# Layer 1's sums begun before the last block ends, and an opening with a place for each image

## The chip, the cores and the metric

The kernel runs on one core of a Trainium2 chip. The metric is the device time of one execution in microseconds (us). A core has TensorE (matrix products and transposes through PSUM), VectorE (DVE), ScalarE (ACT), GpSimd (POOL) and SyncE (SP, which here only issues DMAs). ACT and POOL issue DMAs too; POOL issues the indirect ones, which gather rows by a list of indices.

## The reference

Two graph layers on N = 3327 nodes with D = 128 features (padded to NP = 3328 = 26 blocks of 128 rows), all in float32. The adjacency has about 2% of entries that are not zero (0.0096 made symmetric, and the diagonal).

```
h = relu(layernorm(x))                                   # layer 0: attention, 4 heads
E = leaky_relu(h@w1 [i] + h@w2 [j]);  s = exp(8*tanh(E@a / 8)) * adj
head = leaky_relu((s / sum_j s) @ h @ Wlin.T);  x = x + concat(heads) @ w
h = relu(layernorm(x))                                   # layer 1: a graph convolution
A = adj + I;  dinv = rowsum(A)**-0.5
x = x + relu(dinv[:,None] * A * dinv[None,:] @ (h @ W.T + b))
```

## The kernel before

**Tables.** An opening (L884 to L1062) norms x, multiplies it with the weights and writes, for each node, a row of ROW = 720 floats to DRAM: 64 places for adjacency weights, 128 features, 4 scores, ones, and from PROJ = 208 on 4 x 128 projections. There are two such tables, one for the upper half of a block's rows (hb = 0) and one for the lower (hb = 1); they differ in the first 64 places only, which are rewritten for each block from AT_d, a transposed copy of the adjacency in DRAM (`weights`, L555, issued on SP). The rows are built in `img` tiles, one for four blocks, 7 in all, from a pool of 5 (L952); `store` (L969) writes each to table 0, and to table 1 one image later. The memory of the opening (pool `pre`) is given back at its end, and the gather buffers `g` (pool `pg`, 4 buffers, opened after it) lie there.

**Layer 0** goes through 26 blocks. For each, `prep` (L338) reads 128 rows of the adjacency (`load`, L336, on SP), transposes them on TensorE (L349), copies them out of PSUM on ACT (L351, tile `at`) and writes them to AT_d (L354), and makes on DVE the lists of the neighbours' indices (idx at L442, and idxo at L511 for those that don't fit). Blocks after the first few also multiply the transposed adjacency at once with those columns of layer 1's input that are known by then (`known_step`, L364) into part1_d.

Each half block has 4 windows of 8 gathers (tile `g`, L548) and one of 3 (`ge`). Two groups come out of a window and one out of `ge`, so 18 groups a block. A group is: 16 transposes of gathered projections into PSUM (`z`, L573; in a ge group also L576), a maximum on DVE (L585; on ACT for ge, L582), score products (L597); then, for a window, a copy on ACT (L605), transposes into a `tr` bank (L614; the `tr` pool has two banks), score additions on DVE (L617, L620), tanh and exp on ACT, weights on DVE, and the weighted sums (L645, for ge L663). `close` (L669) ends each half: for the second it goes over L685, L696, L707, L711, L723, L731 and L736, which writes the block's column of layer 1's input into x_sb and sets `closed`.

**The order** of instructions is the order of emission. `slot` (L808) is called 6 times a group; each call takes one step of every open `finish` and `close`, steps of the next block's `prep`, and calls `fetch` and `trickle`. `fetch` queues the gathers of the next window as soon as a buffer is free by the count in `state`; `trickle` issues from this queue at RATE = 0.7 a slot, and each gather is made to wait for the latest maximum of L585 (the pace). POOL does the gathers in order, SP and ACT their DMAs among their other work.

**Layer 1** multiplies x_sb's 26 columns with strips of AT_d, each four blocks (512 rows of the output) wide; strip s starts at column `finished(4*s)` = 4*s - 2 (0 for s = 0), since the columns before are in part1_d. There are 7 strips with 26, 24, 20, 16, 12, 8 and 4 columns, the last one half as wide. Pieces of 11 columns are loaded into g buffers (`strip`, L820, SP and ACT in turn). `layer1` (L859) takes strip after strip, a matmul 128x512 for each column (L870) into a z bank; it takes the first 25 columns of strip 0 between the last steps of the last block, and stops before column 25 until that is written (`yield "all"`). `strip_out` (L841) adds part1, transposes (L853), scales and adds (L854 to L856) and writes the output.

Of the kernel before, what the change touches and what calls it, by code (L numbers as in the profile page):

```python
# [15 lines left out]
P = 128  # L16
# [47 lines left out]
ROW = 720  # L64
FEAT = 64
PROJ = 208
# [161 lines left out]
def _sparse_layers(tc, nc, x, adj, w1, w2, a, wlin, w, gw, gb, gb_sb, gwT, x_sb, dinv, flag, ident, out):  # L228
# [24 lines left out]
    with ExitStack() as l0:  # L253
# [5 lines left out]
        part1_d = dram.tile([D, NP], F32, name="part1_d")  # L259
        NS = -(-NB // 4)  # L260
# [12 lines left out]
        lower = res.tile([P, P], F32, name="lower")  # L273
        rowid = res.tile([P, 1], F32, name="rowid")
# [16 lines left out]
        nc.gpsimd.iota(epos, [[-P, 2 * OVT]], base=2 * NP, channel_multiplier=-1, allow_small_or_imprecise_dtypes=True)  # L291

# [45 lines left out]
        def prep(b, k):  # L338
# [6 lines left out]
            def tables_step(j0):  # L345
# [4 lines left out]
                at = pat.tile([P, 4, P], F32, name="at") if b else blks[0].pool.tile([P, 4, P], F32, name="at0", bufs=4)  # L350
# [65 lines left out]
            hTb = pb.tile([P, P], F32, name="hTb")  # L416
            nc.sync.dma_start(hTb, hT_d[:, b * P:(b + 1) * P])
# [24 lines left out]
            nc.vector.tensor_scalar(idx, pm[:, :64].rearrange("p (c t) -> p c t", c=4), -1.0, float(NP), op0=OP.mult, op1=OP.add)  # L442
# [68 lines left out]
            nc.vector.tensor_scalar(idxo.rearrange("p c t -> p (c t)"), hits, -1.0, float(NP), op0=OP.mult, op1=OP.add)  # L511
# [23 lines left out]
            k.x1b, k.x1n, k.pex, k.hTb = x1b, x1n, pex, hTb  # L535
            yield

        def gather(b, hb, w):

            k = blks[b]  # L540
            tab = tables[hb]
            if w == NW:
                g, n, at = pe_.tile([P, OVT, ROW], F32, name="ge"), OVT, k.idxo[:, hb]
            else:
                g, n, at = pg.tile([P, WT, ROW], F32, name="g"), WT, k.idx[:, w, WT * hb:WT * hb + WT]

            def one(t):
                return nc.gpsimd.indirect_dma_start(out=g[:, t, :], out_offset=None, in_=tab[:, :],  # L548
                                                    in_offset=bass.IndirectOffsetOnAxis(ap=at[:, t:t + 1], axis=0))
# [12 lines left out]
        def stage_z(k, hb, m, slot):  # L562
# [4 lines left out]
            for hp in range(2):  # L567
# [15 lines left out]
                else:  # L583
                    r0 = HALF * hb + 32 * (m % 2)
                    made = nc.vector.tensor_tensor(r.rearrange("p h (i s) -> p h i s", s=16), z.rearrange("p h (i s) -> p h i s", s=16),  # L585
                                            k.x1n[:, 2 * hp:2 * hp + 2, r0:r0 + 32, None].to_broadcast([P, 2, 32, 16]), OP.max)
                    state["pace"] = made.ins.name
# [167 lines left out]
        state["pace"], state["credit"] = None, 0.0  # L755
        RATE = 0.7
        SYNC = mybir.DependencyInfo(mybir.DependencyClass.Sync, mybir.DependencyReason.DATA)
# [12 lines left out]
        def fetch():  # L770
            while state["fetched"] < len(fetches):
# [5 lines left out]
                if b == NB:  # L777
                    strip(*pieces[w])
# [9 lines left out]
        def issue():  # L788

            what, _, _, make = queue.popleft()  # L790
            made = make()
            if what is not None and state["pace"] is not None:
                tc.add_manual_dep(made.ins, state["pace"], SYNC, reason="pace")

        def trickle():
            state["credit"] = min(2.0, state["credit"] + RATE) if queue else 0.0
            while queue and (state["credit"] >= 1 or queue[0][0] is None):
                state["credit"] -= queue[0][0] is not None
                issue()
# [6 lines left out]
        def slot():  # L806
# [6 lines left out]
            trickle()  # L813


        PIECE = 11
        pieces = [(s, j0, min(PIECE, NB - j0)) for s in range(NS) for j0 in range(finished(4 * s), NB, PIECE)]
        strips = {}

        def strip(s, j0, n):  # L820
            g = pg.tile([P, WT, ROW], F32, name="g")
            v = g.rearrange("p t c -> p (t c)")[:, :n * 4 * P].rearrange("p (j i) -> p j i", j=n)
            w = min(4, NB - 4 * s) * P
            for k, lo in enumerate(range(0, n, 4)):
                hi = min(n, lo + 4)
                eng = nc.scalar if k % 2 else nc.sync
                eng.dma_start(v[:, lo:hi, :w], AT_d[s * NP + (j0 + lo) * P:s * NP + (j0 + hi) * P, :w].rearrange("(j p) i -> p j i", p=P))
            strips[s, j0] = v

        def strip_in(s):  # L830
# [6 lines left out]
            if finished(4 * s):  # L837
                nc.sync.dma_start(r1[:, 0], part1_d[:, rows].rearrange("p (b i) -> p b i", b=n))
            return n, rows, r0, r1

        def strip_out(s, po, n, rows, r0, r1):  # L841

            ot, t, xo = r0[:, 1], r1[:, 1], r0[:, 0]
            po = po[:, :n * P].rearrange("p (b i) -> p b i", b=n)
            if finished(4 * s):
                nc.vector.tensor_add(ot, po, r1[:, 0])
            else:
# [10 lines left out]

        def layer1():  # L859
            ending = []  # L860
            for s in range(NS):
                w = min(4, NB - 4 * s) * P
                po = ps_z.tile([P, 2, BANK], F32, name="z")[:, 0]
                j1 = finished(4 * s)
                ins = strip_in(s)
                for j in range(j1, NB):
                    if j == NB - 1 and s == 0:
                        yield "all"
                    at = (j - j1) % PIECE
                    nc.tensor.matmul(po[:, :w], x_sb[:, j, :], strips[s, j - at][:, at, :w], start=(j == j1), stop=(j == NB - 1))  # L870
                    if at == PIECE - 1 or j == NB - 1:
                        allow("g")
                    while ending and next(ending[0], "end") == "end":
                        ending.pop(0)
# [355 lines left out]
```

## Time and profile before

| | |
|---|---|
| time, median of 17 executions | 3149.91 us (3137.22 to 3160.67) |
| the profiled execution | 3138.63 us, span 3136.9 us, mean granted TensorE clock 0.915 |
| busy in the span: PE, DVE, POOL, ACT | 81%, 65%, 57%, 22% |
| DMA | 867.74 MB, 277 GB/s on average; gathers take 65.0% of the 16 engines' time |
| first gather issued, first z transpose | 85.6 us, 89.8 us |
| a steady block, 18 groups | 111.6 us |
| a gather of 128 rows on POOL | 0.976 us busy, one in 1.25 us; landing 4.4 us after its issue (median) |
| a gathered window's last row before its first transpose | 13.5 us (median) |
| last group's z transposes end | 3017 us |
| column 25 of strip 0 | 3051.07 us |
| L870 | 220 records (two a column), 96.4 us busy |

The page shows one execution. Busy time is that of instructions in work, an engine's idle time is put down to what ended it, and the chain of waits is followed back from the last instruction. "Another core or an unknown queue" (remote) stands where the trace doesn't hold the releaser. A granted clock below 1 means that TensorE was throttled in part of that stretch.

### The profile page before, as it was taken

Reading aid. Unit: us, or ns where it says so; the run is one execution under the profiler, and the core shown is the slowest. Engines: PE = TensorE matmul, PEld = TensorE weight load, DVE = VectorE, ACT = ScalarE, POOL = GpSimd, SP = SyncE. Lnnn points to the kernel's source line nnn. Section 1 sums busy time; section 2 is a strip of 40 time slices with the busy share of each in tenths; the row PEclk is TensorE's granted clock in tenths of the full one; section 3 lists DMA queues with packets and bytes.
Section 4 is the critical chain, followed back from the end, with each engine's and each line's share of the span. In section 5 each row is a group of like instructions: output and inputs, shape, how many; then the busy total and the mean of one; then the engine's idle time right before and its main releaser. Section 6 shows DMA issues by size and latency. Waiting matters only on the chain.

```text
span 3136.9 us, 52428 instructions
## 1 busy us (share of the span) xinstructions
PE 2527.3 (81%) x19410; PEld 1751.5 (56%) x19410; DVE 2052.6 (65%) x6256; ACT 691.1 (22%) x1648; POOL 1793.8 (57%) x1865
## 2 busy tenths in 40 slices
PE   5478878878878877888888888788888888887888
PEld 3355555555555555655565565566555556555544
DVE  6466767677677767767676666776666666765432
ACT  3122222122222212222222221222222222221110
POOL 2456665665666666666665656656566555656610
PEclk8799999999999999998999998999899999999899
DMA  9888988898899888888988888888898888988876
GB/s 331 267 284 256 287 289 260 285 296 281 268 287 308 265 286 290 285 262 285 296 264 286 288 253 285 285 275 269 279 283 269 276 286 252 293 257 250 254 254 237
DMA packets 459767, 867.74 MB, mean 277 GB/s; under 512 B 208876, under 2 KB 317936, under 8 KB 456176
## 3 DMA queue, kind: packets, MB, share of 16 engines
q0 software_dynamic: 145600, 671.04, 65.0%
q1 hardware_dynamic: 217360, 136.76, 15.6%
q10 hardware_dynamic: 96544, 56.50, 5.9%
q8 instruction: 156, 2.56, 0.3%
q14 instruction: 107, 0.88, 0.1%
HBM read 795.84 MB, written 112.63 MB: 290 GB/s over the span
## 4 chain that ended last, share of the span: by engine, by line
PE 50%; DVE 11%; another core or an unknown queue 10%; issue 6%; ACT 5%; ACTq 0%; DMA 0%; DVEq 0%
PE z L573 19%; PE s L597 9%; DVE r L585 5%; PE tr L614 4%; PE z L870 3%; PE z L576 3%; PE ag L645 2%; PE ag L663 2%; PE tr L364 2%; ACT r L582 2%; PE tr L349 1%; ACT ssb L605 1%; PE tr L496 1%; PE tr L696 1%
## 5 line engine op out<-in xcount | busy, mean ns | idle before, releaser
L548 POOL DMA_INDIRECT g<-table,idx x1664 | 1623.7, 976 | 1075.9 <-issue 431.9
L573 PE MATMUL z<-ident,g 128*128 128x128 f32 x6656 | 1023.6, 300 | 273.3 <-issue 133.8
L585 DVE TENSOR_TENSOR r<-z,x1n 128x1024 f32<-128x1024 f32 x832 | 1011.4, 1217 | 243.5 <-remote 99.4
L573 PEld LDWEIGHTS z<-ident,g 128*128 128x128 f32 x6656 | 839.5, 155 | 479.3 <-issue 236.1
L597 PE MATMUL s<-r,sel 128*32 128x512 f32 (+1 forms) x3744 | 537.9, 616 | 7.9 <-issue 6.4
L617 DVE TENSOR_TENSOR sc<-tr,g 128x32 f32<-128x32 f32 x208 | 39.4, 190 | 616.7 <-PE tr L614 454.4
L614 PE MATMUL tr<-ident,ssb 128*128 128x128 f32 x988 | 180.5, 309 | 158.5 <-ACT ssb L605 109.1
L605 ACT COPY ssb<-s 128x512 f32<-128x512 f32 x260 | 147.0, 565 | 649.6 <-PE s L597 299.2
L614 PEld LDWEIGHTS tr<-ident,ssb 128*128 128x128 f32 x988 | 124.2, 156 | 195.7 <-ACT ssb L605 138.3
L645 PEld LDWEIGHTS ag<-g,wt 128*32 128x32 f32 x3328 | 112.6, 111 | 191.9 <-issue 179.0
L645 PE MATMUL ag<-g,wt 128*32 128x133 f32 x3328 | 173.2, 282 | 57.2 <-issue 56.4
L399 DVE MAX8 cand<-codes 128x8 f32<-128x52 uint16 x1664 | 215.0, 203 | 0.0
L548 POOL DMA_INDIRECT ge<-table,idxo x156 | 147.5, 946 | 93.9 <-DVE r L585 61.6
L351 ACT COPY at<-tr 128x512 f32<-128x512 f32 (+1 forms) x182 | 101.2, 556 | 330.2 <-remote 122.7
L576 PE MATMUL z<-oi,x1b 128*128 128x384 f32 x416 | 169.7, 488 | 1.6 <-issue 1.4
L597 PEld LDWEIGHTS s<-r,sel 128*32 128x32 f32 x3744 | 81.9, 110 | 149.2 <-issue 126.8
L625 ACT ACTIVATE th<-sc 128x32 f32<-128x32 f32 x260 | 58.1, 224 | 464.0 <-DVE sc L620 170.5
L582 ACT ACTIVATE r<-z 128x768 f32<-128x768 f32 x104 | 84.4, 814 | 296.2 <-remote 131.8
L349 PE MATMUL tr<-ident,adjb 128*128 128x128 f32 x676 | 109.8, 285 | 24.8 <-DMA adjb<-in_adj_dram 10.4
L573 PEld LDWEIGHTS z<-ident,ge 128*128 128x128 f32 x624 | 79.2, 145 | 77.9 <-issue 38.3
L573 PE MATMUL z<-ident,ge 128*128 128x128 f32 x624 | 106.0, 278 | 4.1 <-issue 3.2
L395 DVE SCALAR_TENSOR_TENSOR codes<-adjb,code 128x832 uint16<-128x832 f32 x104 | 102.1, 1018 | 1.4 <-DMA adjb<-in_adj_dram 1.4
(177 smaller groups left out, 2395.0 us busy)
## 6 DMA issues: line engine op xcount, KB each, us to landing
adjb<-in_adj_dram SPq DMA_DIRECT2D x26, 1664.0 KB
table<-AT_d SPq DMA_DIRECT2D x52, 832.0 KB
AT_d<-at ACTq DMA_DIRECT2D x150, 256.0 KB
g<-table,idx POOLq DMA_INDIRECT x1664
table<-img SPq DMA_DIRECT2D x12, 1312.0 KB
g<-AT_d SPq DMA_DIRECT2D x11, 1024.0 KB
g<-AT_d ACTq DMA_DIRECT2D x9, 1024.0 KB
g<-AT_d SPq DMA_DIRECT2D x7, 768.0 KB
```

The source lines that it names most:

```text
L349: nc.tensor.transpose(pt[:, q, :], adjb[:, (j0 + q) * P:(j0 + q + 1) * P], ident)
L395: nc.vector.scalar_tensor_tensor(codes[:, i], adjb[:, c0:c0 + part], 0.0, code[:, c0:c0 + part], op0=OP.not_equal, op1=OP.mult, accum_out= ...
L399: nc.vector.max(cand[:, c, 8:].rearrange("p (r s) -> p r s", s=32)[:, :, sgm % 32], codes.rearrange("p a b -> p (a b)")[:, sgm % 32 * SEG: ...
L548: return nc.gpsimd.indirect_dma_start(out=g[:, t, :], out_offset=None, in_=tab[:, :], in_offset=bass.IndirectOffsetOnAxis(ap=at[:, t:t + 1 ...
L573: nc.tensor.matmul(z[:, i, q * P:(q + 1) * P], g[:, m % 2 * 4 + q, PROJ + h * D:PROJ + (h + 1) * D], ident, is_transpose=True, start=(q == ...
L576: nc.tensor.matmul(z[:, i, :n], k.x1b[:, h * D:(h + 1) * D], k.oi[:, hb * n:(hb + 1) * n], start=False, stop=True, skip_group_check=True)
L582: nc.scalar.activation(r[:, :, :n], z[:, :, :n], AF.Relu)
L585: made = nc.vector.tensor_tensor(r.rearrange("p h (i s) -> p h i s", s=16), z.rearrange("p h (i s) -> p h i s", s=16), k.x1n[:, 2 * hp:2 * ...
L597: nc.tensor.matmul(k.s[32 * h:32 * h + 32, :n], sel[:, h, 31 - at:63 - at], rs[h // 2][:, h % 2, :n], start=(at == 0), stop=(at == 1 or m ...
L605: nc.scalar.copy(ssb[:, :nk * P], s[:, :nk * P])
L614: nc.tensor.transpose(pt[:, q, :], ssb[:, q * P:(q + 1) * P], ident)
L645: nc.tensor.matmul(ag[32 * cg:32 * cg + 32, u, :WORK], wt[:, t].rearrange("p h q -> p (h q)"), g[:, t, FEAT:FEAT + WORK], start=(w == 0 an ...
```

## The change

1. **End of layer 1.** Strips 1, 2 and 3 have their first 12 columns (2 to 13, 6 to 17, 10 to 21) multiplied in advance. The generator `begin` starts with block 24's second half and takes one step a slot. It loads the columns in pairs (18 loads of 512 KB on SP) into the place of the adjacency rows, which no block needs any more, in three thirds; after 14 slots it issues one matmul in four slots into a `tr` bank, which it keeps for the 12 columns of a strip; the sum is copied by ACT and written to part2_d, which `strip_in` reads and `strip_out` adds.
2. **Two strips in front of the last column.** A list of columns in the order of the work replaces the loops: the open columns of strips 0 and 1 up to column 24 (25 + 11), then column 25 of both, then the other strips. Pieces are 11 columns of this list: 7 instead of 13. `strip_in` of the later strips is issued at their fifth column.
3. **Gathers** read up to COLS = 709 instead of 720 floats (PROJ is 197), and for pair t//2 of a window from float 16*(t//2) on, since places before that are not used there. The index is now counted in floats (a constant tile `first`, one iota and one addition).
4. **Pace.** Gathers are issued as soon as they are queued, and wait for no maximum.
5. **g buffers** are four pools of one buffer, taken in turn.
6. **Opening.** Each image has a place of its own; some other tiles of the opening borrow places of the r and ge tiles. Table 1's stores come after all products, in the order of the images, with block 1's rows loaded after the second of them and `weights(0, 1)` after the last; hTb of block 0 is loaded earlier.

```diff
+        def rows_in():
+            state["turn"] += 1
+            return pgs[state["turn"] % 4].tile([P, WT, ROW], F32, name="g")
         def gather(b, hb, w):
-            tab = tables[hb]
+            tab = tables[hb].rearrange("r (c u) -> (r c) u", u=1)
...
-                return nc.gpsimd.indirect_dma_start(out=g[:, t, :], out_offset=None, in_=tab[:, :],
+                lo = 16 * (t // 2) if w < NW else 0
+                return nc.gpsimd.indirect_dma_start(out=g[:, t, lo:COLS], out_offset=None, in_=tab,
...
-            nc.vector.tensor_scalar(idx, pm[:, :64].rearrange("p (c t) -> p c t", c=4), -1.0, float(NP), op0=OP.mult, op1=OP.add)
+            nc.vector.scalar_tensor_tensor(idx, pm[:, :64].rearrange("p (c t) -> p c t", c=4), -float(ROW),
+                                           first[:, None, :].to_broadcast([P, NW, 16]), op0=OP.mult, op1=OP.add)
...
         def issue():
-            what, _, _, make = queue.popleft()
-            made = make()
-            if what is not None and state["pace"] is not None:
-                tc.add_manual_dep(made.ins, state["pace"], SYNC, reason="pace")
+            queue.popleft()[-1]()
         def trickle():
-            state["credit"] = min(2.0, state["credit"] + RATE) if queue else 0.0
-            while queue and (state["credit"] >= 1 or queue[0][0] is None):
-                state["credit"] -= queue[0][0] is not None
+            while queue:
                 issue()
         def slot():
...
+            if state["early"] is not None and next(state["early"], "end") == "end":
+                state["early"] = None
...
+        PAIR = 2
+        BEGUN = 12
+        early = {s: range(finished(4 * s), finished(4 * s) + BEGUN) for s in (1, 2, 3) if finished(4 * s) + BEGUN < NB - 3}
+        def begin():
+            work = [(s, j) for s in early for j in early[s]]
+            pairs = [work[i:i + PAIR] for i in range(0, len(work), PAIR)]
...
+            thirds = pa.tile([P, NP], F32, name="adjb")[:, :3 * PAIR * BANK].rearrange("p (k j i) -> p k j i", k=3, j=PAIR)
+            def bring(k):
+                if k < len(pairs):
+                    for to, of in columns(thirds[:, k % 3], pairs[k]):
+                        nc.sync.dma_start(to, of)
+            for k in range(3):
+                bring(k)
+            for _ in range(14):
+                yield
+            for i, (s, j) in enumerate(work):
+                if j == early[s][0]:
+                    po = bank()
+                nc.tensor.matmul(po, x_sb[:, j, :], thirds[:, i // PAIR % 3, i % PAIR], start=(j == early[s][0]), stop=(j == early[s][-1]))
+                if i % PAIR == PAIR - 1:
+                    bring(i // PAIR + 3)
+                if j == early[s][-1]:
+                    part2 = pv.tile([P, H, P], F32, name="outT").rearrange("p h i -> p (h i)")
+                    nc.scalar.copy(part2, po)
+                    nc.sync.dma_start(part2_d[:, 4 * s * P:4 * s * P + BANK], part2)
+                for _ in range(4):
+                    yield
...
+        front = range(min(2, NS - 1))
+        work = [(s, j) for s in front for j in range(first_column(s), NB - 1)]
+        in_front = len(work)
+        work += [(s, NB - 1) for s in front] + [(s, j) for s in range(len(front), NS) for j in range(first_column(s), NB)]
+        pieces = [work[i:i + PIECE] for i in range(0, len(work), PIECE)]
         def layer1():
+            for i, (s, j) in enumerate(work):
+                if i == in_front:
+                    yield "all"
...
+                nc.tensor.matmul(sums[s][:, :w], x_sb[:, j, :], strips[s, j][:, :w], start=(j == first_column(s)), stop=(j == NB - 1))
...
+            room = [images.enter_context(tc.tile_pool(name=f"image{i}", bufs=1)).tile(
+                        [P, min(4, NB - 4 * i), ROW - FEAT], F32, name=f"img{i}") for i in range(-(-NB // 4))]
...
-                img = pre.tile([P, 4, ROW - FEAT], F32, name="img", bufs=5)
+                img = room[i]
...
                 store(i, 0)
-                if i:
-                    store(i - 1, 1)
...
-                weights(0, 1)
                 turn(0)
+                blks[0].hTb = pb.tile([P, P], F32, name="hTb")
+                nc.sync.dma_start(blks[0].hTb, hT_d[:, :P])
...
-                store(K - 1, 1)
+                for i in range(K):
+                    store(i, 1)
+                    if i == min(1, K - 1) and NB > 1:
+                        load(1)
+                weights(0, 1)
                 advance(NLIST)
                 turn_parameters()
-                if NB > 1:
-                    load(1)
                 advance(NPREP)
-        pg = l0.enter_context(tc.tile_pool(name="pg", bufs=4))
+        pgs = [l0.enter_context(tc.tile_pool(name=f"pg{i}", bufs=1)) for i in range(4)]
...
+                    if (b, hb, m) == (max(0, NB - 2), 1, 0):
+                        state["early"] = begin()
...
-            while ends or tails:
+            while ends or tails or state["early"] is not None:
```

## The prediction

> **What bounds the kernel now.** I read the page's first and fourth part first, then the busy table by stretches, the chain of waits at the end, and the waits and timeline of the opening.
>
> ```profile
> PE 2527.3 (81%) x19410; PEld 1751.5 (56%) x19410; DVE 2052.6 (65%) x6256; ACT 691.1 (22%) x1648; POOL 1793.8 (57%) x1865
> ...
> PE 50%; DVE 11%; another core or an unknown queue 10%; issue 6%; ACT 5%; ACTq 0%; DMA 0%; DVEq 0%
> PE z L573 19%; PE s L597 9%; DVE r L585 5%; PE tr L614 4%; PE z L870 3%; PE z L576 3%; PE ag L645 2%; PE ag L663 2%; PE tr L364 2%; ACT r L582 2%; PE tr L349 1%; ACT ssb L605 1%; PE tr L496 1%; PE tr L696 1%
> ```
>
> TensorE is busiest and half of the chain; DMA stands in it with 0%. So bytes saved in the steady stage buy little by themselves, and TensorE work moved is worth what its new place lets it hide. The busy table (length; then PE, PEld, DVE, ACT, POOL; granted clock, DMA share, GB/s) shows the stages:
>
> ```profile
> 0.00:100.00 100.00, 56.71 (x219) 37.91 (x219) 58.62 (x272) 30.03 (x55) 33.93 (x56) 0.80 0.99 326
> 100.00:200.00 100.00, 60.46 (x448) 41.30 (x448) 52.91 (x169) 15.97 (x34) 52.46 (x56) 0.80 0.80 255
> 2785.00:2896.00 111.00, 91.05 (x721) 61.30 (x722) 68.91 (x166) 22.27 (x57) 69.11 (x73) 0.92 0.84 258
> 2896.00:3000.00 104.00, 81.21 (x621) 53.66 (x619) 48.44 (x94) 16.26 (x44) 63.97 (x68) 0.88 0.82 254
> 3050.00:3137.00 87.00, 76.22 (x198) 35.40 (x198) 18.09 (x31) 0.99 (x2) 0.00 (x0) 0.93 0.67 229
> ```
>
> In the opening the DMA is full and TensorE has 40 us idle in each 100. In the last blocks TensorE is idle about 20 us of 111, DMA at 0.82 to 0.84. After 3050 only layer 1 is left, and TensorE does it without a break. The chain there:
>
> ```profile
> 3045.47 0.91 PE tr L707 x8
> ...
> 3050.61 0.41 ACT x_sb L736
> 3051.07 5.09 PE z L870 x8
> 3056.15 0.44 PE tr L853 x4
> 3056.59 20.60 PE z L870 x48
> 3077.19 0.44 PE tr L853 x4
> 3077.63 17.17 PE z L870 x40
> ...
> 3126.21 0.70 DVE r L854
> ```
>
> From 3051 to 3126 a record of L870 takes 20.60/48 = 0.429 us, and a column (128x512) is two records: **0.858 us**. No piece waits for a strip load.
>
> **The tail.** Before, 25 columns of strip 0 stand ahead of the last block's end and 1+24+20+16+12+8+4 = 85 behind it; the last 4 are half wide, so 83 count. After, 36 columns are done early (three strips of 12), 36 stand in front (25 of strip 0, 11 of strip 1), and 2+8+4+12+8+4 = 38 are left, 36 in full widths. Removed behind the end: 47 x 0.858 = 40.3 us.
>
> Eleven more front columns are 9.4 us. They go between L707 and L736's followers, where the list above has TensorE mostly idle: from the start of L707 at 3045.31 (timeline) to column 25 at 3051.07 are 5.76 us, of which L707, L723 and L731 take 1.05+0.33+0.49; 3.9 us are free. So column 25 comes 5.5 us later (at worst 9.4, since L723 and L731 queue behind columns in TensorE's order). **Tail: -40.3 + 5.5 = -35** (bounds -40 and -31). Strip loads: 74 columns of 256 KB are 19.4 MB; at the 270 GB/s of the stretch 3000 to 3050 this is 72 us, from about 3000 to 3072, while TensorE eats 74 x 0.858 + 6 = 69 us from 3020 to 3089. The supply stays ahead. Strip_out's added DVE additions (three) lie beside columns of the next strip; the last strip has none.
>
> **The early columns.** 36 x 0.858 = 30.9 us of TensorE work go into block 24's second half and block 25, one column in four slots. Bounds: nothing, since 1.5 such stretches have about 34 us of idle TensorE; and 30.9, if all idle time is round trips that no other work shortens. The nearest row is L364, the partial layer-1 sums, which are put singly between groups as well: none in block 1, about 1 us a block in blocks 2 to 5 and 5.2 to 6.8 us in blocks 18 to 23. From one block's last ge transpose to the next one's, blocks 2 to 7 took 110.9 us on average and blocks 18 to 23 113.2: 2.3 us for some 5 us of work, or 0.45. I take 0.45 x 30.9 = **14 us**. Each early strip also holds one of the two `tr` banks for 48 slots. In block 25 only L614 and the close use the other; in block 24's second half block 25's preparation does too. Bounds: nothing, and 9 groups x 1.6 us (L614 to the second score addition); I take 3. The 18 loads of 512 KB stand on SP, past nothing that a block waits for then; the pieces' own loads stand behind them. 9.4 MB over 165 us are 57 GB/s on top of 257: bounds nothing (share 0.82) and 9.4 MB at 285 GB/s = 33 us; I take 2, since gathers land a median 13.5 us ahead of their first transpose. Sum **+19** (bounds 0 and +50).
>
> [...]
>
> **The opening.** Waits between 25 and 85 us, and the timeline around them:
>
> ```profile
> POOL img L953 <- DMA table<-img: 14.1, 2, 7.8
> DVE img L955 <- DMA table<-img: 12.3, 2, 6.8
> ```
> ```profile
> 85.64 1.37 POOL L548 DMA_INDIRECT g<-table,idx  x1 [28.91 <-DVE rel L502]
> ```
> ```profile
> 134.24 1.11 PE L573 MATMUL z<-ident,g 128*128 128x128 f32 x4 [25.45 <-DVE r L585]
> ```
>
> DVE waits 6.8 and 5.5 us for a free image place, and the list of block 0 is behind it: idx is ready at 73.6, yet the first gather goes at 85.6, although L502 has nothing to do with it. It waits for the stores of both tables, since the g buffers lie over the images. After, no image waits, so idx comes 12.3 us earlier, at about 61; table 0's stores (8.73 MB, 22 us at the 395 GB/s reached there) follow the products and end at about 60; the first buffer waits for one image alone. The gathers could start at 62 to 66, some 20 us earlier. But DMA is full until about 133, and the bytes stay the same: table 1's 8.73 MB now run beside the first 35 gathers. What is won is DMA time unused before or filled by gathers at their issue rate (368 KB per 1.25 us = 294 GB/s instead of 395): 52 us (table 0 under way) + 23.6 MB (table 1 8.7, its weights 0.9, block 1's rows 1.7, 35 gathers 12.3) at 350 to 370 GB/s = 116 to 119 us for what ended at 133. I take **-14**. Bounds: -24 (all of the earlier start) and +10 (the copies at L351, which wait up to 20.0 us for their turn beside a full DMA, held half as long again). weights(0,1) and table 1 are needed by the second half's first gather, at 151.6 before; cover is ample. Added here: a GpSimd iota, a memset an image, a DVE constant: under 2 us on engines that wait anyway.
>
> **The steady stage.** Gathers lose 140 of 2880 bytes on average (4.9%), and none waits for a DVE maximum (POOL's waits for that: 132.9 and 61.6 us). The data are 13.5 us early already, and TensorE is not seen waiting for gathers. Against it: eight gathers now go as a burst of 10 us, beside which the adjacency writes and loads run; ACT's copies at L351 waited 123 us in all, 32 in the opening. Bounds over 25 blocks: -25 and +50 (about 1 and 2 us per block). I take 0, by the chain's DMA 0%. The changed index instruction is one of 0.22 us a block.
>
> **Sum**: -35 + 19 - 14 + 0 = **-30 us**. Against the profiled execution (span 3136.9, 3138.6 with what lies around it) that is 3108.6. That execution is among the fastest of the 17; their median is 3149.9, and against it the sum gives 3120, my forecast.
>
> **Rivals.**
> 1. *The bursts slow the steady stage* (slower). Without pacing each freed buffer is refilled at 1.25 us a gather; the copies at L351 then wait behind gather packets as in the opening, ACT is in order, and the score copy L605 behind it holds TensorE. Price 2 us x 25 = +50: 3170. It decides from 1.2 us per block. For it: the 20.0 us wait in the opening. Against: pacing at 0.7 a slot spread eight gathers over only 12 us.
> 2. *The early strips are paid in full* (no change). 30.9 + 3 + 10 to 20 for gathers pushed back are 44 to 54, against 35 + 14 = 49: 3145 to 3155. For it: chain PE 50%. Against: 34 us of idle.
> 3. *DMA relief counts* (faster still). With fewer bytes the waits put down to an unknown queue (10%) shorten by 1 us a block, and the early columns hide: 3120 - 25 - 10 = 3085.
> 4. *The opening doesn't do what it says*: its stall at 108.8 to 134.2 is set by the full DMA and stays: 3134.
>
> **How the numbers follow.** Forecast 0.53, rival 1 0.13, rival 2 0.11, rival 3 0.16, rival 4 0.07. A measurement tells about 0.2% from no change, here 3143.6 to 3156.2. The range takes in the forecast, rivals 2, 3 and 4, and leaves out most of rival 1: 3083 to 3157. The forecast's own range is 3104 to 3138. Faster: 0.53 + 0.16 + 0.07 and a fifth of rival 2 = 0.78; same: the larger part of rival 2 = 0.07; slower: 0.13 + 0.02 = 0.15.
>
> **What would show it.** Right: about 38 columns (76 records) of z between the last x_sb and the end, in 35 us; blocks 24 and 25 together 15 to 25 us longer; first gather before 70 us; steady blocks at 111.6 us. Wrong: blocks of 113 and more with longer waits at L351's place; TensorE waiting for g in the last blocks; the gap after 108 us as long as before; TensorE waiting for strips in the tail.

## The result, and the profile after

The changed kernel takes **3234.2 us** (median; 3222.4 to 3241.5 in 8 runs) against 3149.28 us before (47 runs): a ratio of **1.0268** (95% interval 1.0252 to 1.0285). It is slower by 85 us where the prediction said faster by 30. Its profiled execution took 3212.5 us (span 3210.5), 74 us above that of before, so the stages below explain 74 us.

The split is by the start of the last z transpose of a block's second ge group (L573 before, L587 after), in us from the span's start:

| | before | changed | difference | forecast |
|---|---|---|---|---|
| start to end of block 0 | 226.14 | 218.65 | -7.5 | -14 |
| blocks 1 to 5 | 561.5 | 563.8 | +2.3 | 0 |
| blocks 6 to 23, mean of one | 112.0 | 117.2 | 18 x 5.14 = +92.6 | 0 |
| blocks 24 and 25 | 211.6 | 230.1 | +18.5 | +19 |
| from there to the end | 121.0 | 88.7 | -32.3 | -35 |

Two terms of the sum came out as numbers (the early columns and the tail), the opening gave half, and the steady stage, put at nothing, lost 95 us. The page's busy line and chain, after:

```profile
PE 2562.9 (80%) x19410; PEld 1745.0 (54%) x19410; DVE 2050.4 (64%) x6260; ACT 689.9 (21%) x1651; POOL 1795.2 (56%) x1873
...
PE 54%; DVE 15%; another core or an unknown queue 13%; issue 8%; ACT 7%; DMA 3%; POOL 1%; ACTq 0%; DVEq 0%; SPq 0%; POOLq 0%
```

No engine has more instructions (eight more at most), and only TensorE is busy for clearly longer, by 36 us. The two pages' chains can't be set side by side: the shares of before add up to 82%, since that chain could be followed back only to 540 us. In blocks 7 to 23, which both chains cover, the unknown releasers' part grows from 252 to 308 us, DVE's from 256 to 307 and ACT's from 118 to 157, while TensorE's shrinks from 1114 to 1054. The groups show where the idle time is (busy and mean of one, then the idle time before them and its main releaser); first the kernel before, then the changed one:

```profile
L548 POOL DMA_INDIRECT g<-table,idx x1664 | 1623.7, 976 | 1075.9 <-issue 431.9
L585 DVE TENSOR_TENSOR r<-z,x1n 128x1024 f32<-128x1024 f32 x832 | 1011.4, 1217 | 243.5 <-remote 99.4
```
```profile
L562 POOL DMA_INDIRECT g<-table,idx x1664 | 1623.6, 976 | 1117.6 <-PE ag L658 557.3
L599 DVE TENSOR_TENSOR r<-z,x1n 128x1024 f32<-128x1024 f32 x832 | 1011.3, 1217 | 392.9 <-remote 208.5
```

The maximum costs the same 1.217 us, but DVE waits 150 us longer for its input. GpSimd waits for buffers (the weighted sums, L658) for 557 us; before, it waited 125 us for them (L645) and 133 for the pace. The gathers are early, not late: the last row of a window landed 17.3 us (median) before the first transpose of its group, against 13.5 before.

Busy time over 17 blocks, from some 10 us into block 7 on, before and after (length; PE, PEld, DVE, ACT, POOL; clock, DMA share, GB/s):

```profile
908.00:2815.00 1907.00, 1572.96 (x12598) 1119.55 (x12598) 1316.07 (x4013) 438.15 (x1056) 1158.83 (x1191) 0.92 0.88 278
```
```profile
906.00:2903.00 1997.00, 1601.87 (x12606) 1118.81 (x12608) 1314.13 (x4013) 436.54 (x1056) 1159.14 (x1192) 0.92 0.82 255
```

The same instructions take 90 us longer at the same mean clock and with the DMA less loaded. Two of TensorE's waits grow most in that stretch, the one for the maximum and the one for ACT's copy of the transposed adjacency (in all, times, longest), before and after:

```profile
PE z L573 <- DVE r L585: 48.0, 37, 5.3
PE tr L364 <- ACT at L351: 28.7, 13, 4.0
```
```profile
PE z L587 <- DVE r L599: 99.7, 109, 5.2
PE tr L370 <- ACT at L357: 71.7, 28, 6.6
```

The opening after, GpSimd's timeline and then TensorE's:

```profile
66.87 1.17 POOL L562 DMA_INDIRECT g<-table,idx  x1 [23.85 <-DVE miss L491]
...
89.72 0.94 POOL L562 DMA_INDIRECT g<-table,idx  x1 [12.52 <-ACT at L357]
```
```profile
127.69 1.11 PE L627 MATMUL tr<-ident,ssb 128*128 128x128 f32 x4 [19.55 <-issue]
```

The index list is ready at 60.2 us and the first gather goes at 66.9, close to the 62 to 66 worked out. But the second buffer waits until 89.7, and a TensorE stall of 19.6 us stands where one of 25.5 was. The profile names a copy on ACT for the buffer's wait; in a run of the same opening (e10, below) it names the stores of the tables:

```profile
90.05 0.95 POOL L562 DMA_INDIRECT g<-table,idx  x1 [11.93 <-DMA table<-img]
```

The tail, the chain after the last block's L720 and then TensorE's timeline:

```profile
3152.19 0.89 PE tr L720 x8
3153.08 3.44 PE z L937 x8
3156.63 4.29 PE z L937 x10
3160.92 0.22 PE tr L744 x2
3161.14 0.86 PE z L937 x2
3162.02 3.79 PE z L937 x8
...
3168.45 2.31 DMA out_dram<-r
...
3171.94 4.14 DMA r<-part_d
```
```profile
3177.77 0.89 PE L913 MATMUL tr<-ident,r 128*128 128x128 f32 x4 [3.36 <-DVE r L906]
```

TensorE no longer waits for x_sb: the 11 columns fill the close, and column 25 comes 10.0 us after L720's start (by the timeline, 3152.03 to 3162.02) instead of 5.8. One wait is new: the transposes of a later strip wait 3.4 us, since its input tiles are loaded only after an earlier strip's output store has landed. -40.3 + 4.2 + 3.4 = -32.7 stand against -32.3 measured.

### The profile page after: what moved, and what is told of

The parts are those of the page before. It is cut to its first block, busy times and chain, and to the rows that moved or that the text cites. A ratio compares the mean times of both kernels' runs of the same rounds, so it can differ in the third digit from the quotient of the medians.

```text
span 3210.5 us, 51974 instructions
## 1 busy us (share of the span) xinstructions
PE 2562.9 (80%) x19410; PEld 1745.0 (54%) x19410; DVE 2050.4 (64%) x6260; ACT 689.9 (21%) x1651; POOL 1795.2 (56%) x1873
## 4 chain that ended last, share of the span: by engine, by line
PE 54%; DVE 15%; another core or an unknown queue 13%; issue 8%; ACT 7%; DMA 3%; POOL 1%; ACTq 0%; DVEq 0%; SPq 0%; POOLq 0%
PE z L587 19%; PE s L610 9%; DVE r L599 8%; PE z L590 4%; PE tr L627 4%; PE ag L676 2%; ACT r L596 2%; PE tr L355 2%; PE z L937 2%; PE tr L370 2%; ACT ssb L618 2%; DMA g<-table,idx 2%; PE ag L658 1%; DVE cand L405 1%
## 5 line engine op out<-in xcount | busy, mean ns | idle before, releaser
L599 DVE TENSOR_TENSOR r<-z,x1n 128x1024 f32<-128x1024 f32 x832 | 1011.3, 1217 | 392.9 <-remote 208.5
L587 PE MATMUL z<-ident,g 128*128 128x128 f32 x6656 | 1025.1, 298 | 283.0 <-DVE r L599 141.0
L587 PEld LDWEIGHTS z<-ident,g 128*128 128x128 f32 x6656 | 829.8, 153 | 530.4 <-DVE r L599 239.4
L618 ACT COPY ssb<-s 128x512 f32<-128x512 f32 x260 | 147.3, 566 | 725.2 <-PE s L610 342.5
L658 PE MATMUL ag<-g,wt 128*32 128x133 f32 x3328 | 201.4, 280 | 85.6 <-issue 84.6
L658 PEld LDWEIGHTS ag<-g,wt 128*32 128x32 f32 x3328 | 123.1, 110 | 234.6 <-issue 226.3
L370 PE MATMUL tr<-at,x_sb 128*128 128x128 f32 x488 | 79.9, 308 | 91.6 <-ACT at L357 72.0
L370 PEld LDWEIGHTS tr<-at,x_sb 128*128 128x128 f32 x488 | 66.4, 209 | 116.2 <-ACT at L357 92.6
L355 PE MATMUL tr<-ident,adjb 128*128 128x128 f32 x676 | 112.1, 289 | 18.7 <-DMA adjb<-in_adj_dram 10.3
L587 PEld LDWEIGHTS z<-ident,ge 128*128 128x128 f32 x624 | 78.0, 143 | 70.0 <-issue 34.7
```

Of the source, the lines that this page charges most:

```text
L355: nc.tensor.transpose(pt[:, q, :], adjb[:, (j0 + q) * P:(j0 + q + 1) * P], ident)
L370: nc.tensor.matmul(pq[:, :P], x_sb[:, j0 + q, :], at[:, q, :], start=(q == 0), stop=(q == js[-1]))
L587: nc.tensor.matmul(z[:, i, q * P:(q + 1) * P], g[:, m % 2 * 4 + q, PROJ + h * D:PROJ + (h + 1) * D], ident, is_transpose=True, start=(q == ...
L618: nc.scalar.copy(ssb[:, :nk * P], s[:, :nk * P])
L658: nc.tensor.matmul(ag[32 * cg:32 * cg + 32, u, :WORK], wt[:, t].rearrange("p h q -> p (h q)"), g[:, t, FEAT:FEAT + WORK], start=(w == 0 an ...
```

## The experiments

All are edits of the changed kernel unless it is said otherwise. Theories at first: **A**, the unpaced gathers slow the steady blocks; **B**, the shorter rows do; **C**, the four pools of one buffer do.

**e1, pace back.**
```diff
         def issue():
-            queue.popleft()[-1]()
+            what, _, _, make = queue.popleft()
+            made = make()
+            if what is not None and state["pace"] is not None:
+                tc.add_manual_dep(made.ins, state["pace"], SYNC, reason="pace")
         def trickle():
-            while queue:
+            state["credit"] = min(2.0, state["credit"] + RATE) if queue else 0.0
+            while queue and (state["credit"] >= 1 or queue[0][0] is None):
+                state["credit"] -= queue[0][0] is not None
                 issue()
```


> The changed kernel with the pace back: at most 0.7 gathers a slot, and each gather waits for the latest maximum on DVE, as in the kernel before; all else as changed. From the traces so far, a block from 6 to 23 takes 117.2 us after the change and 112.0 before (18 blocks, 93 us), the opening is 7 us shorter, the last two blocks 18 us longer and the tail 32 us shorter. Theory A (gathers issued in bursts slow the steady blocks): blocks of 112 us, the whole some 90 us under the changed kernel, about 3140. Theory B (the shorter rows, which start and end off a multiple of 64 bytes and put the projections at byte 788, slow them): no change, about 3230. Theory C (four pools of one buffer instead of one of four): no change, about 3230.

**e2, whole rows.**
```diff
-COLS = 709
-PROJ = 197
+COLS = 720
+PROJ = 208
-                lo = 16 * (t // 2) if w < NW else 0
+                lo = 0
```


> The changed kernel with whole rows gathered: 720 floats for every index, projections at place 208 again, the constant added to the indices the same for all; pace, pools, opening and end as changed. Theory A (bursts): blocks of 117 us or a little more, since the bursts carry 5 per cent more bytes; about 3235. Theory B (short rows): blocks of 112 us, about 3140. Theory C (pools): about 3230.

**e3, one pool.**
```diff
-            return pgs[state["turn"] % 4].tile([P, WT, ROW], F32, name="g")
+            return pgs[0].tile([P, WT, ROW], F32, name="g")
-        pgs = [l0.enter_context(tc.tile_pool(name=f"pg{i}", bufs=1)) for i in range(4)]
+        pgs = [l0.enter_context(tc.tile_pool(name=f"pg{i}", bufs=4)) for i in range(1)]
```


> The changed kernel with one pool of four g buffers in place of four pools of one; all else as changed. Theory A (bursts) and theory B (short rows): steady blocks stay at 117 us; the first gather waits for all images again, so the opening is some 7 us longer, about 3237. Theory C (pools): blocks of 112 us, about 3150.

**e5, e1 and e2 together.**

> The changed kernel with the pace back and whole rows gathered; four pools, opening and end as changed. If A or B or both together make the loss, blocks are at 112 us and the whole at about 3140, some 10 us under the kernel before. If it stays near 3230 with blocks of 117 us, neither pace nor rows did it, and what is left is the pools or something that the opening set up for the later blocks.

Measured on one chip, before at 3151.5:

| | us | ratio (95%) | end of block 0 | a block, 6 to 23 | blocks 24, 25 | tail |
|---|---|---|---|---|---|---|
| e1, pace | 3113.1 | 0.987 (0.982 to 0.992) | 215.1 | 112.6 | 223.9 | 88.4 |
| e2, whole rows | 3225.8 | 1.023 (1.014 to 1.031) | 218.8 | 117.1 | 235.8 | 87.2 |
| e3, one pool | 3252.6 | 1.031 (1.026 to 1.036) | 234.6 | 117.9 | 233.2 | 86.8 |
| e5, both | 3119.9 | 0.989 (0.984 to 0.994) | 213.0 | 113.1 | 224.1 | 88.5 |

Theory A holds, B and C fall: the pace alone brings the blocks back to 112.6 us, and e1 beats both kernels. The short rows are worth at most some 7 us under the pace (e1 against e5, two executions each). The four pools are worth 16 us in the opening: with one pool the first gather goes at 91.1 us instead of 66.9, and the opening would have been a loss.

**e6 and e7, half of the pace each; e8, no early columns (under the pace).** e6 keeps e1's `trickle` and leaves out the wait, e7 keeps the wait and empties the queue at once.
```diff
-        early = {s: ... for s in (1, 2, 3) if finished(4 * s) + BEGUN < NB - 3}
+        early = {s: ... for s in () if finished(4 * s) + BEGUN < NB - 3}
```


> The changed kernel with half of the pace: a gather is put into GpSimd's program at most 0.7 times a slot, so that the adjacency weights' DMAs on SP and all waits stand in the order of the paced kernel, but no gather waits for a maximum of DVE. GpSimd does nothing else in these blocks, so it can still issue a gather as soon as its buffer is free. Theory A1 (the time at which gathers go, that is the burst itself): no gain, blocks 6 to 23 at 117 us, about 3225. Theory A2 (the order of the program: where SP's weights stand and which DMA shares a semaphore with which): blocks at 112.6 us, about 3115.

> The other half of the pace: gathers are put into GpSimd's program as soon as they are queued, as in the changed kernel, but each waits for the latest maximum of DVE at that place. Theory A1 (the time of the gathers): most of the gain is back, if the wait holds the first gather of a window until the maximum; the other seven still follow at once, so blocks of 113 to 116 us, 3125 to 3190. Theory A2 (the order of the program): no gain, about 3230.

> The paced kernel without the early columns: strips 1 to 3 wholly in layer 1, the 11 columns of strip 1 in front and everything else as in the paced kernel, which took 3113 us with its last two blocks at 223.9 us and a tail of 77.1 (from the last group's transposes to the end). By the prediction the early columns cost 19 us in the last blocks and save 36 x 0.858 = 31 us of tail: last two blocks 205 to 212, tail about 108, about 3128. If the early columns are hidden wholly: last two blocks 224, about 3144.

These fell on another chip, and there the kernel before takes **2570.3 us**, not 3150. e6 took 2531.9 (0.985; 0.981 to 0.989), e7 2535.0 (0.987; 0.983 to 0.990), e8 2555.1 (0.994; 0.991 to 0.996). e8 answers its question: without early columns the last two blocks take 177.7 us and the tail 114.0, with them (e6) 187.3 and 88.3. They cost 9.6 and save 25.6; in e18 below, the whole pace on the other chip of that speed, the last two blocks take 184.0. (The expectation of e8 counts the tail from 11 us later than the tables here: its 77.1 is their 88.4.)

**e9 to e12: changed, e1, e6 and e7 side by side.** The same four programs, to have them on one chip.

> The changed kernel, unaltered, beside its three paced forms on one chip, since the last three runs fell on a chip where the kernel before takes 2570 us and not 3150, its blocks 90 us and not 112, and no run of the changed kernel stands there. Theory A (the unpaced gathers cost): on a chip like the first, 1.024 of the kernel before and 1.037 of the paced kernel; on a chip like the second it tells whether the loss belongs to the chip. If it belongs to the chip: 2530 there, like the half-paced forms.

> The paced kernel once more, on the same chip as the changed one. On a chip like the first 0.987 of the kernel before. On a chip like the second, where the half-paced forms are at 2532 and 2535: between 2525 and 2540.

> Half of the pace, the order of the program alone, on the same chip. On a chip like the first: Theory A1 (the time at which gathers go) about 1.024 of the kernel before, theory A2 (the order of the program) 0.988. On a chip like the second 2532 again.

> The other half of the pace, the wait alone, on the same chip. On a chip like the first: theory A1 0.99 to 1.01 of the kernel before, theory A2 1.024. On a chip like the second 2535 again.

On the chip of e1 to e5 (before 3162.1): changed 3223.7 (1.020; 1.008 to 1.031), paced 3108.2 (0.983; 0.972 to 0.994), credit alone 3225.0 (1.020), wait alone **3378.9** (1.069; 1.052 to 1.085). A block from 6 to 23: 117.3, 112.4, 117.3 and 122.5 us. The credit alone changes nothing, so the order of the program is not the cause (A2 falls); the time at which gathers go is. But A1 in its simple form falls too: holding each window's gathers to one maximum is worse than no pace at all. Each half needs the other. My reading, which no run shows by itself: the credit spreads the gathers over the slots, and the wait makes that spread real in time.

The credit-alone program ran on both kinds of chip. Seventeen blocks again, on the first kind and on the second (e6):

```profile
911.00:2910.00 1999.00, 1601.91 (x12597) 1116.71 (x12597) 1314.26 (x4012) 436.17 (x1056) 1158.30 (x1191) 0.92 0.81 255
```
```profile
734.00:2270.00 1536.00, 1411.26 (x12586) 1006.96 (x12584) 1297.12 (x4011) 446.46 (x1054) 1167.19 (x1192) 0.99 0.99 332
```

The same instructions in 1536 instead of 1999 us: DVE, ACT and POOL are busy for the same time within 3%, TensorE for 12% less, at a clock of 0.99 instead of 0.92, and with a DMA share of 0.99 instead of 0.81. On the second kind DMA and GpSimd leave the block little room (70 gathers x 1.25 us = 87.5 of 90 us); on the first kind something else sets its time. One stall of the first kind (e11) shows what it looks like, on TensorE and then on ACT:

```profile
1318.18 0.60 PE L355 MATMUL tr<-ident,adjb 128*128 128x128 f32 x4
...
1327.54 1.11 PE L627 MATMUL tr<-ident,ssb 128*128 128x128 f32 x4 [4.30 <-ACT ssb L618]
```
```profile
1325.88 0.58 ACT L357 COPY at<-tr 128x512 f32<-128x512 f32 x1 [8.73 <-remote]
```

L355's transposes begin at 1318.2 and end 0.6 us later by the profile, which models these ends, but ACT copies them only at 1325.9; ACT's score copy L618 stands behind, and TensorE waits 4.3 us for that. On the second kind (e6) this copy waits 7.1 us less. TensorE's own semaphore shows what the copy waits for: between 300 and 2900 us, all 18 such copies with an unknown releaser in the kernel before, and all 16 in the changed one, start 23 or 24 ns after an update of it. In its records, updates whose modelled ends follow one after the other stay away for some us (by the earliest end, below, 3.0 on average before and 3.3 after) and then come together (three within 0.12 us at 1313.7 in e11). I counted such **pauses** between 300 and 2300 us of each execution: an update over 1.5 us after the one before it and over 1.2 us after a modelled end. The records have holes: of the updates that TensorE's instructions should make in that time, the traces of the first kind hold 80 to 93%, those of the second 99% or more. So the count depends on the end that an update is set against. The table gives it for the earliest end since the last update, and for the nearest end before the update (in brackets those over 4 us). It takes in e13 to e16, which follow below and ran on another chip of the first kind.

| first kind of chip | pauses, earliest end | nearest end | maximum, idle | half-clock time | spread of gathers | a block, 6 to 23 |
|---|---|---|---|---|---|---|
| before | 224 (38) | 103 (29) | 99 | 300 | 69 | 112.0 |
| e10, paced | 227 (34) | 97 (33) | 77 | 304 | 63 | 112.4 |
| changed | 227 (55) | 106 (11) | 209 | 283 | 78 | 117.2 |
| e11, credit alone | 222 (59) | 102 (9) | 209 | 287 | 78 | 117.3 |
| e12, wait alone | 208 (35) | 126 (33) | 245 | 382 | 84 | 122.5 |
| e14, before without pace | 202 (67) | 131 (19) | 306 | 290 | 81 | 120.4 |
| e15, rate 1.0 | 195 (47) | 131 (36) | 318 | 372 | 83 | 123.6 |
| e16, rate 0.66 | 233 (31) | 112 (11) | 130 | 324 | 65 | 115.5 |
| e13, spaced | 109 (15) | 0 | none | 413 | 52 | 117.7 |

(Maximum, idle: VectorE's idle time before L585 or L599 that the page puts down to no known releaser, in us of the whole run. Half-clock time in us of the 2000. Spread: the standard deviation of the gathers' GB/s in stretches of 5 us.)

On the second kind there are 0 or 1 pauses in 2000 us (4 in e17), no wait for an unknown releaser, and 17 to 38 us at half clock (352 in e17). What holds by every count: paced or not, late completions are common on the first kind and all but absent on the second (e13 is taken up below), and the idle time before the maximum that nothing explains goes with the loss, 77 and 99 us at a pace of 0.7, 209 to 318 without the pace, with half of it or at a rate of 1.0. What doesn't hold is that the unpaced kernels have longer pauses: by the earliest end they have more of over 4 us, by the nearest end fewer. The changed kernel has no more half clock than the one before; e12 and e15 have.

**e13 to e16.** e13 writes an unused tile twice after each gather on GpSimd; e14 is the kernel **before** with the pace taken out; e15 and e16 are e1 with RATE 1.0 and 0.66.
```diff
+                made = nc.gpsimd.indirect_dma_start(...)
+                for _ in range(2):
+                    nc.gpsimd.memset(pad, 0.0)
+                return made
```


> The changed kernel, no pace, but GpSimd writes a small unused tile (128x128) twice after each gather, so that gathers stand some 1.5 to 1.7 us apart instead of 1.25, whatever DVE does. If it is the density of the gathers in time that slows the blocks, the steady blocks come down from 117.2 toward 112.5 us, 3115 to 3160. If the gathers must stand behind a DVE maximum, that is at a certain place within a group, nothing is gained: 117 us and 3225 or, if GpSimd has become the bound (70 gathers at over 1.6 us), slower still.

> The kernel before with the pace alone taken out: neither credit nor wait; rows, pool, opening and end as before. If the pace alone made the loss: blocks 6 to 23 at 116 to 118 us, all in all 75 to 115 us over the kernel before, 3225 to 3265. If the loss needs another part of the change beside it: within 20 us of the kernel before.

> The paced kernel at one gather a slot instead of 0.7, each still behind the latest maximum. If it is the density of the gathers: between the paced kernel's 112.5 us a block and the changed kernel's 117.2, some 114 to 116, 3135 to 3175. If the wait on the maximum is what counts: 112.5, 3110.

> The paced kernel at 0.66 gathers a slot, just above the 70 gathers in 108 slots (0.648) that a block needs. Density: the same as at 0.7 or slightly better, 3095 to 3115. If gathers come too late for their transposes at times: slower, with TensorE waiting for g.

On a third chip, of the first kind (before 3191.5): e13 3240.5 (1.013; 1.008 to 1.019), **e14 3325.1** (1.040; 1.032 to 1.047), e15 **3398.7** (1.063; 1.057 to 1.069), e16 3184.9 (0.997; 0.994 to 1.000). e14 is the plainest proof: the pace alone, taken out of the old kernel, costs 134 us (blocks of 120.4). e15 shows that a wait at a higher rate is as bad as the wait alone (blocks of 123.6, and 122.5 in e12): the rate has to fit the need. e16, 2% above the need of 0.648 a slot, gained less against the kernel before than 0.7 did on the first chip (0.983 and 0.987); 0.7 was not run on this one. Three expectations were missed: e14 cost more than 75 to 115 us, e15 fitted neither alternative, and e16 came out above 3095 to 3115. e13 doesn't tell density from place (below).

**e17 to e19: shorter writes, with e1 and the changed kernel beside it.**

> The changed kernel with GpSimd writing an unused tile (128x128, then 128x48) after each gather: in the first spaced run two writes of 0.24 us made 1.6 us from gather to gather, and at 70 gathers (112 us and more) GpSimd became the bound: gathers landed 0.6 us after their first transpose was due. Here it is some 1.45 us, 102 us a block, so that the gathers stay ahead. Density theory: blocks between the paced kernel's and the changed kernel's, nearer the paced, ratio to the kernel before 0.985 to 1.005. Place theory (a gather has to stand behind a DVE maximum of its own slot): like the changed kernel, 1.02 to 1.03.

> The paced kernel, in three rounds beside the changed one: the best version of this study. 0.983 to 0.989 of the kernel before by the two runs so far.

> The changed kernel, unaltered, as the measure for the spaced run on the same chip: 1.02 to 1.03 of the kernel before.

The chip was of the second kind (before 2570.2): e17 3127.3 (1.217; 1.214 to 1.219), e1 2530.2 (**0.985**; 0.983 to 0.986), changed 2534.4 (**0.986**; 0.983 to 0.988). TensorE's longest wait in e13 and then in e17, between 910 and 2815 us, shows what the spacing did:

```profile
PE z L591 <- DMA g<-table,idx: 350.6, 268, 6.6
```
```profile
PE z L591 <- DMA g<-table,idx: 324.5, 247, 5.6
```

GpSimd's gathers come too late in both: at 1.6 and 1.5 us each, 70 of them take 112 and 106 of the blocks' 117.7 and 113.3 us, and the last row of a window lands up to half a us after the first transpose of its group has started (medians). So neither tells density from place. On the second kind the 0.3 us more for each gather cost everything (1.217 against 0.986); on the first kind they cost nothing against the changed kernel (1.013, and 1.020 to 1.027 for that one on other chips).

e13 shows one thing more. It ran on the chip of e14 to e16, and its trace holds no wait for an unknown releaser; counted by the nearest end it has no pause. So the late completions don't come with the chip alone: by that count they were gone when the gathers stood 1.6 us apart with GpSimd writing between them. Which of the two did it, no run tells.

## Why the prediction was wrong

**The steady stage** is the step that failed: "I take 0, by the chain's DMA 0%". The sum put the pace's removal at nothing; blocks 6 to 23 took 5.1 us more each, 95 us with blocks 1 to 5. With the pace back 4.6 of the 5.1 are gone (e1), and without it the old kernel loses 134 us (e14). The reason given did not carry: gathers that hardly end a wait in the chain (0.1% of blocks 7 to 23 before, 1.1% after) cost 87 us of blocks 1 to 23 by when they were issued (the changed kernel against e1). One reading behind it was wrong too: the copies at L351 waited 330 us in all; the 123 were the part without a known releaser.

**Rival 1** had the right sign, the point of decision (1.2 us a block) was passed, and half of its path was there. It said that the copies at L351 would wait longer and hold up TensorE. In blocks 7 to 23 their waits grew from 208 to 249 us, and TensorE's wait for them from 28.7 to 71.7 us (e10: 26.7). What it had wrong is what they would wait for. The adjacency writes did not fall behind gather packets: from issue to landing they took 4.46 us (median) before, 3.74 after and 4.2 to 4.3 under the pace, so they were faster in the slow kernel. The copies' waits without a known releaser grew, from 70.5 to 124.6 us, and those for a DMA only from 2.2 to 4.7. TensorE's wait for the maximum grew by 52 us beside it, which no rival had. "Pacing spread eight gathers over only 12 us" was my argument against it; it was no argument, since e14 lost 4% with just that spread gone.

**The tail** was right: -32.3 for -35. Column 25 was 4.2 us later, not 5.5; missed were the 3.4 us for the input tiles. Strip loads kept ahead, as worked out: after column 25 the timeline has no TensorE wait for one.

**The early columns** met their number by luck: +18.5 for +19, but that holds the loss of the unpaced gathers too, which the sum had at nothing. Under the pace they cost 12.3 (e1), and 6 to 10 on the second kind of chip (e18 and e6 against e8). TensorE waited for no gather beside the early loads: in blocks 24 and 25 of the changed kernel, at a DMA share of 0.81 and 0.82, the list of waits holds none. On the second kind, at a share of 0.97 (e6), TensorE waits 2.0 us there for gathers and 3.5 us for the early loads. So no run shows rival 2's 10 to 20 us for gathers pushed back.

**The opening** gave 7.5 (11 to 12 under the pace) for 14. The image waits went and the first gather came at 66.9, just behind the 62 to 66 of the forecast. The step that fell short is the drain of the DMA: the second buffer waited until 89.7, at a DMA share of 0.95 in the first 100 us (0.99 before), and the stall after it, rival 4's, was 19.6 us long after 25.5.

**Rivals 2 and 3** did not come about: no 30.9 us were lost in the last blocks, and fewer bytes bought 0.5 us a block (e1 against e5), not 1.

On the second kind of chip, with at most 1 pause in 2000 us for these kernels, the changed kernel is 36 us faster than the one before, near the 30 of the sum, and the pace makes no difference clear of noise there (2530 against 2534). No profile of the kernel before comes from that kind, so this can't be split by stage, and the agreement may be luck. The assumption failed on the chip whose profile I had, and that profile had its warning: the waits for unknown releasers (10% on the page, 13% of blocks 7 to 23), which I left unexplained and priced only in rival 3, as a gain.

What stays open: what makes TensorE's completions late on the first kind of chip, and how unpaced gathers turn that into lost time. The spread goes with the loss in most kernels of the table, but that is a correlation, and e13 and e16 don't fit it; both runs with evenly spaced gathers and no wait were bound by GpSimd, so it wasn't tried cleanly. Nor does a run tell whether the two kinds are the chips' own or come from something that ran beside the kernel: four chips are on record, each in one or two rounds.

## What to carry to other kernels

A pace that waits for nothing you can see in the chain may be worth more than any other edit of a change (134 us in e14, against 32.3 for the tail): take it out alone and measure, before you count other gains on top. Split a change by stage (here by each block's last transpose): a shorter opening and a shorter end were hidden under one bad edit, and with that edit undone the kernel is at 0.983 to 0.987 of the old one. Before you compare two chains, see how far back each could be followed. And where a profile has long waits without a releaser (10% of the chain here), put an unknown of that size into the range.

## What the runs showed of the hardware

The same program took 23 to 24% more on some chips than on others (3151 to 3191 against 2570 for the kernel before). In seventeen blocks of one program (e11 against e6) VectorE, ScalarE and GpSimd were busy for the same time within 3%, TensorE for 14% longer at a lower clock (0.92 against 0.99). On the first kind, in all kernels of the table but e13, updates of TensorE's semaphore came late against the modelled ends some 10 to 12 times in 100 us by the earliest end, by 3.0 us on average in the kernel before and 3.3 in the changed one (by the nearest end 5 to 7 times, by 3.0 and 2.6 us). The records give half clock for 14 to 21% of the time in all nine. On the second kind there were 0 or 1 late ones in 2000 us (4 in e17), and half clock for 1 to 2% of the time, but for 18% in e17, where TensorE waited 324.5 us for gathers.

In the kernel before, 104 of the 107 half-clock stretches in the records last 3.41 us (70), 6.83 (33) or 10.24 (1), in the changed one 97 of 100 (64, 26 and 7). No run shows what begins such a stretch or sets its length. The late completions are not these stretches: of the 103 that the kernel before has by the nearest end, 79 lie wholly in time that the records give at full clock.

A verdict can turn with the chip: 1.027 on one kind, 0.986 on the other. The paced version was faster on both (0.983 to 0.987, and 0.985).
